# A transformer block with attention over channels and a gated convolution: strips without side columns, and the variance's epsilon on GpSimd

## The chip, the cores and the metric

The kernel runs on one core of one Trainium2 chip. The metric is the device time of one execution in microseconds (us). The engines are named as the profile names them: PE is TensorE (PEld its weight loads), DVE is VectorE, ACT is ScalarE, POOL is GpSimd, SP is SyncE, which only issues DMAs. All data is float32; one float32 matmul stands as two instructions in the trace.

## The reference, cut to what matters

`x` is 16 x 128 x 96 x 96 (batch, channels, height, width). Both LN weights are ones and both LN biases zeros in the data, but the kernel uses them as given.

```python
x_hwc = x.transpose(0, 2, 3, 1)
xn1 = _layernorm(x_hwc, ln1_w, ln1_b)            # over the 128 channels of a pixel, eps 1e-5
attn_out = _attention(xn1, wq, wk, wv, wp)       # 8 heads of 16 channels: a 16x16 matrix per head
x = x + attn_out.transpose(0, 3, 1, 2)
xn2 = _layernorm(x.transpose(0, 2, 3, 1), ln2_w, ln2_b).transpose(0, 3, 1, 2)
# _ffn: 1x1 conv 128 -> 512, depthwise 3x3 conv with zero padding, exact gelu, 1x1 conv 512 -> 128
x = x + _ffn(xn2, w_in, w_dw, w_out)
```

The attention normalizes q and k over all 9216 pixels, so it needs only the Gram matrix of the normalized pixels of an image; after that the whole attention is one 128x128 matrix and a column, applied to each pixel.

## The kernel before, in words

The images are worked through one after the other, the first norm of the next image overlapping the second half of this one. Pixels come in batches of four 128x128 tiles (576 batches in all: 18 of each image for the first norm `a`, 18 for the second norm `b`). For a batch, `forth` (L716) transposes the pixels on TensorE into one of two PSUM buffers (`tr`), `stats` (L723) takes mean and variance sums on VectorE, `variance` (L730) on ScalarE divides the sum by the 128 channels and adds epsilon, `power` (L734) on GpSimd raises to -1/2, `scaled` (L759) on ScalarE multiplies and writes the tile `zT`, `gram` (L768, first norm only) adds to the Gram matrix, `back` (L802) transposes back into the one buffer `bk`, and `place` (L805) copies it into a ring `xn` of rows. The mean is taken out in the weights. `attention` (L852 on) makes the 128x128 matrix, `mix` (L665) applies it.

The feed-forward part goes by blocks of 16 rows, 96 in all, and by four chunks of 128 hidden channels. For the first three chunks (`conv_job`) TensorE makes the hidden rows (`hidden`, L976), ScalarE keeps them with a bias (`kept`, L979), and the nine taps of the depthwise convolution are shared out: six on VectorE (`tap`, L1006, a scalar_tensor_tensor with two inputs in SBUF), two as products on ScalarE (`product`, L999) that DMAs issued by GpSimd add up (`add_products`, L1013), the centre tap in the first instruction. Then comes gelu (L1017).

The fourth chunk does the same in 25 blocks, and in the other 71 (`by_matmuls`, three blocks of four) the whole convolution runs on TensorE. There `split` (L1083) makes strips: for each of four groups of 32 channels, the four quarters of a PSUM bank hold odd or even rows and the left or right half of the width, nine rows of 49 columns and one column of the image's outer side, 50 columns in all. The outer column, and rows outside the image, are filled by matmuls of minus the bias (L1085). `kept` (L1092) copies all 450 columns to SBUF, and `conv` (L1105) multiplies by diagonal 64x32 tap matrices, four groups by two halves at a time. The tile `h1_3` is used for both kinds of block; when the kind goes from matmuls to taps, `around` (L439, L440) on GpSimd writes the zeros that the taps need.

`ffn_out` (L1139) multiplies back to 128 channels, ScalarE evicts (L1149), and a DMA adds to the output. All four PSUM banks `h` are shared by `hidden`, `split`, `conv`, `mix` and `ffn_out`.

The order of every engine's instructions is made ahead by `Plan`: each piece of work has an engine, a cost in ns, and a place (a number of jobs plus an offset of its kind from the table `AT`), and a simulated clock hands out the work that is ready in the order of places. `SLACK` is added to what a result takes to reach another engine, `STEP` spreads the pieces of one kind. On each engine the instructions then run in that fixed order, each waiting for its semaphores.

Of the kernel before, what the change touches and what calls it, by code (L numbers as in the profile page):

```python
# [39 lines left out]
    load_1=-318.45, load_2=250.75, tables=-176.75, weights=-199.9, zeros=280.85, pads=489.4, pads_0=-50.0,  # L40
    load_a=-397.35, forth_a=-242.55, stats_a=-48.4, variance_a=52.55, power_a=346.4, scaled_a=65.85,
    gram=-109.85, back_a=-291.7, place_a=163.65, attention=-399.95, mix=-263.75, residual=-1.05, mixed=-9.75,
    add_x=163.65, forth_b=-248.0, stats_b=-54.25, variance_b=-72.2, power_b=-242.45, shift_b=-65.25,
    scaled_b=519.65, back_b=-664.1, place_b=430.4, evicted=-175.6, add_out=-299.05, halo=332.2, hidden=-67.95,
    kept=-6.5, products=623.75, add_last=230.4, tap=-40.35, add_first=521.3, gelu=615.7, split=-72.5,
    packed=65.05, conv=-64.0, conv_gelu=-632.25, out=-63.65, add=699.15, store=57.0, mix_0=-629.3,
    residual_0=-0.45, mixed_0=1.1, add_x_0=-191.4, gram_0=425.2, forth_a_0=-164.1, forth_b_0=-555.1,
    stats_a_0=-203.2, stats_b_0=31.65, scaled_a_0=166.35, scaled_b_0=435.1, back_a_0=198.1, back_b_0=63.05,
    place_a_0=213.65, place_b_0=-41.2, shift_b_0=-104.65, late=436.35, store_x2=-259.8, store_x2_0=-280.3,
    variance_a_0=296.05, variance_b_0=-572.0, power_a_0=446.6, power_b_0=-200.95, attention_0=-700.85,  # L50
    load_a_0=-699.6, hidden_0=-343.05, kept_0=688.75, products_0=-317.3, tap_0=406.55, add_last_0=-476.1,
    add_first_0=-25.55, gelu_0=-695.0, split_0=-310.35, packed_0=-61.1, conv_0=-522.45, conv_gelu_0=2.7,
    out_0=-354.3, evicted_0=38.2,
# [3 lines left out]
STEP = dict(scaled=1.089, hidden=0.115, products=-0.129, tap=-0.536, split=2.985, conv=0.6, out=0.866)  # L57
SLACK = dict(PE=450, DVE=120, ACT=130, POOL=410, ADD=200, MOVE=360)
# [5 lines left out]
T_VARIANCE = 190  # L64
# [4 lines left out]
class Plan:  # L69
# [45 lines left out]
    def order(self):  # L115
# [39 lines left out]
        def dispatch(engine, time):  # L155
# [40 lines left out]
            elif engine == "POOL":  # L196
                rest = self.two - time
                ns, result = (ns, result) if rest <= 0 else (rest + ns - 143, rest + result - 143)
                own = result
# [49 lines left out]
def tile_restormer_block(  # L249
# [68 lines left out]
    def column(t, v):  # L318
# [5 lines left out]
    whole = const.tile([P, 1], F32, name="whole")  # L324
    nbeta = const.tile([P, P], F32, name="nbeta")
# [20 lines left out]
    SW, SR = W // 2 + 2, BR // 2 + 1  # L346
    PART = SR * SW
    h1s = [
        h1p.tile([P, (BR + 2) * WP + 2 if n != PE_CHUNK else 4 * PART], F32, name=f"h1_{n}") for n in range(NCH)
# [95 lines left out]
    def packed(k):  # L445
        return strips(h1s[PE_CHUNK][:, k * PART : (k + 1) * PART])
# [8 lines left out]
    def weights(p):  # L455
# [8 lines left out]
        def loads_1():  # L464
# [7 lines left out]
            v["col"] = t[:, 10 * P + Q : 10 * P + Q + 24].rearrange("p (a t) -> p a t", a=2)  # L472
            v["by_part"] = t[:, 11 * P : 11 * P + 48]
            v["nb"] = t[:, 11 * P + 48 : 11 * P + 49]
# [74 lines left out]
        def keep_in_centred():  # L549
            nc.scalar.copy(winT.rearrange("p n c -> p (n c)"), v["in_a"])  # L550
            nc.scalar.copy(beta, v["in_b"][:, P : P + NCH])

        def column_of():
# [20 lines left out]

        def diagonals():
            nc.vector.tensor_copy(v["by_part"], v["spread"])
# [72 lines left out]
    def norm(i, second, place_of):  # L649
# [49 lines left out]
        def pixels(s, m):  # L699
# [27 lines left out]
            def variance():  # L727
                d["mv"] = d["st"].rearrange("p j (t v) -> p (j t) v", v=3)
                ve = d["ve"] = small.tile([P, QB * QT], F32, tag="ve", name=f"ve_{name}_{m}")
                nc.scalar.activation(ve, d["mv"][:, :, 2], AF.Copy, scale=1.0 / C, bias=EPS)  # L730

            def power():
                rstd = d["rstd"] = small.tile([P, QB * QT], F32, tag="rstd", name=f"rstd_{name}_{m}")
                nc.gpsimd.tensor_tensor(rstd, d["ve"], mhalf, ALU.pow)  # L734
# [43 lines left out]
            act(T_VARIANCE, at("variance" + ab, s, i), variance, [(*bt, "s")], [(*bt, "r")])  # L778
# [45 lines left out]
    def attention(s, i):  # L824
# [26 lines left out]
        def _():  # L851
            nc.scalar.copy(sb([P, P + 1], "gs"), grams[i][:, : P + 1])  # L852
# [92 lines left out]
        def _():  # L945
            nc.scalar.copy(sb([P, P], "mwT", keep), v["ps_m"])
# [105 lines left out]
    def by_matmuls(p, g):  # L1052
# [15 lines left out]
        def split(k):  # L1068
            ph = d["ph", k] = bank((g, "split", k), PART)
            w = slice(k * Q, (k + 1) * Q)  # L1070
            todo, sides = [], []
            for q in range(4):
# [3 lines left out]
                for e in (*range(k0), *range(k1, SR)):  # L1076
                    sides.append(to[:, e, :])
                sides.append(to[:, k0:k1, half * (SW - 1)])
                lo, hi = (0, W // 2 + 1) if half == 0 else (W // 2 - 1, W)
                for e, (e0, m, z) in enumerate(strided(r0 - 1 + y + 2 * k0, k1 - k0)):  # L1080
                    todo.append((e, q, to[:, k0 + e0 : k0 + e0 + m, 1 - half : SW - half], z[:, :, lo:hi]))
# [166 lines left out]
```

## Time and profile before

| | |
|---|---|
| median of 3 runs | 3908.28 us (3907.63 to 3912.27) |
| the profiled execution | 3905.63 us, span 3903.9 us |
| TensorE busy | 3797.5 us, 97% |
| VectorE busy | 3695.5 us, 95% |
| ScalarE busy | 3618.6 us, 93% |
| GpSimd busy | 1858.0 us, 48% |
| granted TensorE clock, mean | 0.996 |

The span is the time from the first to the last instruction. A row of a group reads: line, engine, operation, what it writes and reads, how many, then busy time and mean duration in ns, then the idle time of the engine before them and what ended it. A row of the waits reads: who waited, for whom, the total in us, how often, the longest. A row of the timeline reads: start, duration, engine, line, operation, and in brackets the idle time before it. A GpSimd instruction's duration includes the time that it waits for the memory port.

### The profile page before, as it was taken

To read this page: it belongs to the slowest core of one execution; us is meant where nothing else is said; L and a number is where in the kernel's file an instruction comes from. 1 tells how busy PE (TensorE), PEld (TensorE's weight loads), DVE (VectorE), ACT (ScalarE), POOL (GpSimd) and SP (SyncE) were. 2 spreads that over 40 slices of the span, in tenths; PEclk is the share of its full clock that TensorE was granted. 3 is DMA by queue.
4 is the path that set the end of the run, shared out by engine and by line. 5 is a ranking of instruction groups with operands and counts; after the bars stand their busy time and mean duration, and the time that the engine had idled before them with its cause. 6 is when DMAs were issued, how large, how long until landed. Compare 5 with 4: busy or idle time off the path is not lost.

```text
span 3903.9 us, 81207 instructions
## 1 busy us (share of the span) xinstructions
PE 3797.5 (97%) x32452; PEld 2337.7 (60%) x32452; DVE 3695.5 (95%) x3310; ACT 3618.6 (93%) x7473; POOL 1858.0 (48%) x1586
## 2 busy tenths in 40 slices
PE   8899999999999999999999999999999999999998
PEld 6556656566565665656556565665656656666544
DVE  6998999999999999999999999999999999999998
ACT  6899999999999999999999999999999999899995
POOL 4445555354454545545445454544545444454431
PEclk9999999999999999999999999999999999999999
DMA  5899999999999999999999999999999999999997
GB/s 145 174 200 224 193 211 210 200 223 190 218 201 203 221 191 222 196 206 218 186 214 202 208 217 190 224 199 211 216 184 223 203 213 206 195 221 192 205 186 161
DMA packets 188921, 790.94 MB, mean 203 GB/s; under 512 B 21888, under 2 KB 23424, under 8 KB 188544
## 3 DMA queue, kind: packets, MB, share of 16 engines
q0 software_dynamic: 130608, 633.92, 83.7%
q1 hardware_dynamic: 57936, 151.83, 10.8%
q8 instruction: 256, 4.19, 0.4%
q14 instruction: 121, 0.99, 0.1%
HBM read 150.62 MB, written 149.42 MB: 77 GB/s over the span
## 4 chain that ended last, share of the span: by engine, by line
PE 58%; ACT 15%; DMA 10%; DVE 9%; issue 4%; POOL 3%; POOLq 0%; ACTq 0%; DVEq 0%; SPq 0%
PE h L1139 15%; PE h L976 12%; PE h L1105 10%; DMA h<-h 8%; DVE h L1006 8%; PE h L665 4%; PE g L768 4%; ACT h L999 4%; PE h L1083 4%; ACT h L979 3%; ACT zT L759 3%; PE pB_b L802 2%; PE pT_b L716 2%; PE pB_a L802 2%; ACT h L1017 2%
## 5 line engine op out<-in xcount | busy, mean ns | idle before, releaser
L1006 DVE SCALAR_TENSOR_TENSOR h<-h,ratio,h 128x1520 f32<-128x1520 f32 (+1 forms) x1567 | 2750.3, 1779 | 13.7
L1013 POOL DMA_DIRECT2D h<-h x624 | 589.7, 964 | 1045.3 <-ACT h L999 416.6
L1139 PE MATMUL h<-h,woutT 128*128 128x384 f32 x3072 | 1059.6, 489 | 11.1 <-ACT h L979 7.0
L999 ACT ACTIVATE h<-h,ratio 128x1536 f32<-128x1536 f32 (+1 forms) x624 | 1012.4, 1638 | 2.4 <-DMA h<-h 1.3
L976 PE MATMUL h<-xn,winT 128*128 128x384 f32 (+3 forms) x2466 | 947.8, 500 | 31.5 <-ACT h L1149 13.2
L1139 PEld LDWEIGHTS h<-h,woutT 128*128 128x128 f32 x3072 | 570.7, 191 | 389.5 <-issue 21.2
L979 ACT ACTIVATE h<-h,beta 128x384 f32<-128x384 f32 (+1 forms) x1204 | 734.1, 659 | 26.4 <-PE h L976 19.8
L734 POOL TENSOR_TENSOR rstd_a<-ve_a,mhalf 128x4 f32<-128x4 f32 x288 | 545.0, 1895 | 360.3 <-ACT ve_a L730 347.6
L734 POOL TENSOR_TENSOR rstd_b<-ve_b,mhalf 128x4 f32<-128x4 f32 x288 | 528.9, 1841 | 345.6 <-ACT ve_b L730 334.2
L1006 DVE SCALAR_TENSOR_TENSOR h<-h,ratio 128x1536 f32<-128x1536 f32 x313 | 567.0, 1812 | 95.8 <-ACT h L979 94.7
L1105 PE MATMUL h<-h,taps 64*32 64x384 f32 x13632 | 584.7, 484 | 2.3 <-ACT h L979 2.3
L976 PEld LDWEIGHTS h<-xn,winT 128*128 128x128 f32 x2466 | 419.0, 190 | 232.6 <-ACT h L1149 26.6
L1017 ACT ACTIVATE h<-h 128x1536 f32<-128x1536 f32 (+1 forms) x316 | 484.5, 1534 | 32.6 <-DMA h<-h 31.8
L1105 PEld LDWEIGHTS h<-h,taps 64*32 64x32 f32 x13632 | 251.0, 106 | 288.5 <-issue 260.2
L759 ACT ACTIVATE zT<-pT_b,rstd_b 128x128 f32<-128x128 f32 x1132 | 338.0, 440 | 9.3 <-POOL rstd_b L734 8.4
L759 ACT ACTIVATE zT<-pT_a,rstd_a 128x128 f32<-128x128 f32 x1080 | 319.8, 421 | 18.1 <-POOL rstd_a L734 18.0
L768 PE MATMUL g<-zT 128*128 128x129 f32 x2160 | 286.8, 275 | 3.9 <-ACT zT L759 3.9
L665 PE MATMUL h<-xn,mwT 128*128 128x384 f32 x768 | 279.2, 490 | 3.2 <-ACT x L674 2.9
L768 PEld LDWEIGHTS g<-zT 128*128 128x128 f32 x2160 | 263.7, 191 | 6.7 <-ACT zT L759 4.3
L1149 ACT COPY h<-h 128x384 f32<-128x384 f32 x376 | 201.3, 535 | 60.9 <-PE h L1139 60.2
L1083 PE MATMUL h<-xn,winT 128*32 128x441 f32 (+4 forms) x2464 | 250.4, 507 | 1.7 <-ACT h L1113 1.7
L723 DVE BATCH_NORM_STATS2 st_b<-pT_b 128x6 f32<-128x256 f32 x566 | 211.9, 419 | 28.4 <-PE pT_b L716 19.3
(190 smaller groups left out, 3776.3 us busy)
## 6 DMA issues: line engine op xcount, KB each, us to landing
h<-h POOLq DMA_DIRECT2D x520, 768.0 KB, 9.5
h<-h POOLq DMA_DIRECT2D x104, 720.0 KB, 10.5
x<-in_x_dram SPq DMA_DIRECT2D x192, 384.0 KB, 7.5
out_dram<-x SPq DMA_DIRECT2D x190, 384.0 KB, 9.3
x<-in_x_dram POOLq DMA_DIRECT2D x189, 384.0 KB, 9.2
out_dram<-h POOLq DMA_DIRECT2D x94, 768.0 KB, 10.7
out_dram<-x SPq DMA_DIRECT2D x4, 192.0 KB, 1.9
h<-in_L_conv_w_in_dram SPq DMA_DIRECT2D x1, 256.0 KB, 2.7
```

Source lines behind the costliest of these rows:

```text
L665: nc.tensor.matmul(rows(pm), lhsT=mats[i][0], rhs=interior(i, u), start=True, stop=True)
L734: nc.gpsimd.tensor_tensor(rstd, d["ve"], mhalf, ALU.pow)
L759: nc.scalar.activation(zT(q)[:, k, :P], d["pT", q][:, k, :], AF.Copy, scale=d["rstd"][:, t : t + 1])
L768: nc.tensor.matmul(grams[i][:, : P + 1], lhsT=zt[:, :P], rhs=zt, start=(q == 0 and k == 0), stop=(q == NU * TPU // QT - 1 and k == QT - 1),)
L976: nc.tensor.matmul(rows(ph)[:, k : k + m, :], lhsT=winT[:, n, :], rhs=z, start=True, stop=True)
L979: nc.scalar.activation(window(h1_, r, e - r, 1), rows(d.pop(("ph", r))), AF.Identity, bias=beta[:, n : n + 1])
L999: nc.scalar.activation(d["pr", t][:, o0:o1, :], shifted(t, o0, o1), AF.Copy, scale=ratio[:, n, t : t + 1])
L1006: nc.vector.scalar_tensor_tensor(h3[:, o0:o1, w0:w1], shifted(t, o0, o1, w0, w1), ratio[:, n, t : t + 1], onto, ALU.mult, ALU.add)
L1013: nc.gpsimd.dma_start(out=to[:, o0:o1, :], in_=d["pr", t][:, o0:o1, :], accum_op=ALU.add)
L1017: nc.scalar.activation(h3, h3, AF.Gelu)
L1105: nc.tensor.matmul(halves(d["pc", y, c][k * Q : (k + 1) * Q, :]), lhsT=taps[cs, k, 6 * y + t, :], rhs=packed(k)[cs, up : up + SR - 1, dx : ...
L1139: nc.tensor.matmul(rows(d["po"]), lhsT=woutT[:, n, :], rhs=h3s[g, n][:, s * UR : (s + 1) * UR, :], start=(k == 0), stop=(k == NCH - 1),)
```

## The change

The strips lose their outer column: `SW` is 49, `split` fills nine rows of 49 with no side matmuls, and the copies move 441 columns. In SBUF the rows of a part stand 50 apart and share one side column between the end of a row and the start of the next; that column holds minus the bias and is written by GpSimd (`sides`, four instructions of 128x10) each time the kind of block goes from taps to matmuls, 25 times. Of 1320 matmuls with minus the bias, 184 remain, for rows outside the image.

The variance step is now a GpSimd instruction of 128x4 ahead of the power, 576 of each. It only adds 128 times epsilon to the sum of squares; the missing division by 128 is made up by factors in the weights and in the copies of the attention, where one copy becomes two (16 instructions more on ScalarE). Costs, slacks and all places in the tables are new, and so is the order on every engine.

```diff
-    SW, SR = W // 2 + 2, BR // 2 + 1
-    PART = SR * SW
+    SW, SR = W // 2 + 1, BR // 2 + 1
+    PART = SR * (SW + 1) + 1
...
-    def packed(k):
-        return strips(h1s[PE_CHUNK][:, k * PART : (k + 1) * PART])
+    def packed(k, r, n, at_, m):
+        o = k * PART + r * (SW + 1) + at_
+        return h1s[PE_CHUNK][:, o : o + n * (SW + 1)].rearrange("p (r w) -> p r w", w=SW + 1)[:, :, :m]
+
+    def sides():
+        for k in range(4):
+            nc.gpsimd.tensor_scalar(
+                h1s[PE_CHUNK][:, k * PART : (k + 1) * PART : SW + 1], ones_row[:, : SR + 1], npad[:, k : k + 1], None, ALU.mult
+            )
...
             def variance():
                 d["mv"] = d["st"].rearrange("p j (t v) -> p (j t) v", v=3)
-                ve = d["ve"] = small.tile([P, QB * QT], F32, tag="ve", name=f"ve_{name}_{m}")
-                nc.scalar.activation(ve, d["mv"][:, :, 2], AF.Copy, scale=1.0 / C, bias=EPS)
+                rstd = d["rstd"] = small.tile([P, QB * QT], F32, tag="rstd", name=f"rstd_{name}_{m}")
+                nc.gpsimd.tensor_scalar(rstd, d["mv"][:, :, 2], C * EPS, None, ALU.add)
 
             def power():
-                rstd = d["rstd"] = small.tile([P, QB * QT], F32, tag="rstd", name=f"rstd_{name}_{m}")
-                nc.gpsimd.tensor_tensor(rstd, d["ve"], mhalf, ALU.pow)
+                nc.gpsimd.tensor_tensor(d["rstd"], d["rstd"], mhalf, ALU.pow)
...
-            act(T_VARIANCE, at("variance" + ab, s, i), variance, [(*bt, "s")], [(*bt, "r")])
+            op("POOL", T_VARIANCE, at("power" + ab, s, i), variance, [(*bt, "s")], [(*bt, "r")], T_VARIANCE, T_VARIANCE)
...
-            nc.scalar.copy(sb([P, P + 1], "gs"), grams[i][:, : P + 1])
+            gs = sb([P, P + 1], "gs")
+            nc.scalar.activation(gs[:, :P], grams[i][:, :P], AF.Copy, scale=float(C))
+            nc.scalar.activation(gs[:, P:], grams[i][:, P : P + 1], AF.Copy, scale=C**0.5)
...
-                sides.append(to[:, k0:k1, half * (SW - 1)])
-                lo, hi = (0, W // 2 + 1) if half == 0 else (W // 2 - 1, W)
+                lo, hi = (0, SW) if half == 0 else (W - SW, W)
...
-            nc.scalar.copy(packed(k), strips(d.pop(("ph", k))))
+            nc.scalar.copy(packed(k, 0, SR, 1, SW), strips(d.pop(("ph", k))))
...
-                if not by_pe(g):
-                    pool(300, at("pads", first[g], g >= HEAD), lambda: around(h1s[PE_CHUNK]), [], [*whole_h1, ("pk",)])
+                change = sides if by_pe(g) else lambda: around(h1s[PE_CHUNK])
+                pool(700 if by_pe(g) else 300, at("pads", first[g], g >= HEAD), change, [("w", "conv")], [*whole_h1, ("pk",)])
...
-SLACK = dict(PE=450, DVE=120, ACT=130, POOL=410, ADD=200, MOVE=360)
+SLACK = dict(PE=9, DVE=228, ACT=4, POOL=453, ADD=949, MOVE=44)
```

What this moves on the engines is seen in the order of their instructions. On TensorE before, in the middle of an image, a pair of strips (here written to the banks h_76 and h_78), its side matmuls, and what follows:

```order
L768 MATMUL g_3279<-zT_150 128x129 x4
L1083 MATMUL h_76<-xn,winT 32x9x49 x4
L1085 MATMUL h_76<-ones_row,nbeta 32x9 x4
L1083 MATMUL h_78<-xn,winT 32x9x49 x4
L1085 MATMUL h_78<-ones_row,nbeta 32x9 x4
L858 MATMUL g_3279<-wqkT,gs_4674 128x256
```

and at such a place in the changed kernel, where both pairs of a block follow each other:

```order
L1093 MATMUL h_79<-xn,winT 32x441 x4
L1093 MATMUL h_78<-xn,winT 32x441 x4
L1093 MATMUL h_76<-xn,winT 32x441 x4
L1093 MATMUL h_77<-xn,winT 32x441 x4
L1149 MATMUL h_79<-h_12_146,woutT 128x384
```

The side matmuls are gone, and the next work stands right behind the strips.

On GpSimd before, in the second norm (`rstd_b` are its powers, the DMAs with `h` add the products of taps, L677 adds x, L1153 adds to the output):

```order
L734 TENSOR_TENSOR rstd_b_2_9442<-ve_b_2_9439,mhalf 128x4
L1013 DMA h_7_140<-h_6_139 128x1440
L677 DMA x_4_5_9434<-in_x_dram 128x768
L734 TENSOR_TENSOR rstd_b_3_9475<-ve_b_3_9469,mhalf 128x4
L1153 DMA out_dram<-h_8_141 128x1536
L734 TENSOR_TENSOR rstd_b_4_9520<-ve_b_4_9516,mhalf 128x4
```

and after, where both norms and the four instructions of `sides` (L452) meet:

```order
L740 TENSOR_SCALAR rstd_b_8_5075<-st_b_8_5062 128x4
L743 TENSOR_TENSOR rstd_b_8_5075<-rstd_b_8_5075,mhalf 128x4
L687 DMA x_2_9_5066<-in_x_dram 128x768
L452 TENSOR_SCALAR h_3_133<-ones_row,npad 128x10 x4
L1024 DMA h_10_144<-h_1_135 128x1440
L1024 DMA h_0_134<-h_13_147 128x1536
L740 TENSOR_SCALAR rstd_a_1_5143<-st_a_1_5136 128x4
L743 TENSOR_TENSOR rstd_a_1_5143<-rstd_a_1_5143,mhalf 128x4
```

Each power now has an instruction ahead of it that waits for the statistics themselves, mostly with nothing between the two, and two DMAs of tap products stand behind the four sides.

More of the change, by code (lines that the diff above doesn't have):

```diff
@@ L45 @@
[L45 to L49, printed above, removed]
@@ new lines @@
+    gram=210.95, back_a=-266.95, place_a=-700.0, attention=-230.4, mix=39.5, residual=-1.05, mixed=395.6,
+    add_x=-48.55, forth_b=146.8, stats_b=-444.3, variance_b=-72.2, power_b=219.9, shift_b=-65.25,
+    scaled_b=-160.4, back_b=-668.3, place_b=144.05, evicted=-688.8, add_out=83.65, halo=692.3, hidden=317.1,
+    kept=-136.65, products=412.4, add_last=-539.35, tap=-104.2, add_first=-440.95, gelu=249.75, split=-194.25,
+    packed=-622.2, conv=321.6, conv_gelu=-402.05, out=323.9, add=-349.15, store=116.65, mix_0=-436.95,
@@ L56 @@
 Q = 32
-STEP = dict(scaled=1.089, hidden=0.115, products=-0.129, tap=-0.536, split=2.985, conv=0.6, out=0.866)
-SLACK = dict(PE=450, DVE=120, ACT=130, POOL=410, ADD=200, MOVE=360)
+STEP = dict(scaled=0.202, hidden=0.107, products=0.662, tap=0.151, split=-0.021, conv=1.084, out=-0.853)
+SLACK = dict(PE=9, DVE=228, ACT=4, POOL=453, ADD=949, MOVE=44)
 NORM1_END = 6.0
@@ L197, in dispatch @@
                 rest = self.two - time
-                ns, result = (ns, result) if rest <= 0 else (rest + ns - 143, rest + result - 143)
-                own = result
+                if rest > 0:
+                    ns, result, own = rest + ns - 143, rest + result - 143, rest + own - 143
             if o[9]:
@@ L324, in tile_restormer_block @@
     whole = const.tile([P, 1], F32, name="whole")
+    npad = const.tile([P, NCH], F32, name="npad")
     nbeta = const.tile([P, P], F32, name="nbeta")
@@ L342, in tile_restormer_block @@
     h1p = ctx.enter_context(tc.tile_pool(name="h1p", bufs=1))
-    SW, SR = W // 2 + 2, BR // 2 + 1
-    PART = SR * SW
+    SW, SR = W // 2 + 1, BR // 2 + 1
+    PART = SR * (SW + 1) + 1
     h1s = [
-        h1p.tile([P, (BR + 2) * WP + 2 if n != PE_CHUNK else 4 * PART], F32, name=f"h1_{n}") for n in range(NCH)
+        h1p.tile([P, (BR + 2) * WP + 2 if n != PE_CHUNK else 4 * PART + 4], F32, name=f"h1_{n}") for n in range(NCH)
     ]
@@ L945, in _ @@
         def _():
-            nc.scalar.copy(sb([P, P], "mwT", keep), v["ps_m"])
+            nc.scalar.activation(sb([P, P], "mwT", keep), v["ps_m"], AF.Copy, scale=C**0.5)
             nc.scalar.copy(sb([P, 1], "d", keep), v["ps_d"])
@@ L1068, in split @@
         def split(k):
[L1069 removed]
+            ph = d["ph", k] = bank((g, "split", k), SR * SW)
             w = slice(k * Q, (k + 1) * Q)
[L1071 removed]
+            todo, outside = [], []
             for q in range(4):
```

50 lines of the change are left out of this document (26 added, 24 removed).

## The prediction

> **What bounds the kernel now.** I read the head of the page first, then the busy time in four stretches, then the waits of TensorE. The page's head gives the span and the work of each engine.
>
> ```profile
> span 3903.9 us, 81207 instructions
> PE 3797.5 (97%) x32452; PEld 2337.7 (60%) x32452; DVE 3695.5 (95%) x3310; ACT 3618.6 (93%) x7473; POOL 1858.0 (48%) x1586
> ```
>
> Three engines are nearly full, so the average cannot say which one sets the pace. The stretches can (start, end and length, then the busy time of each engine, the granted clock and the share of the DMA engines):
>
> ```profile
> 0.00:170.00 170.00, 141.93 (x1024) 98.59 (x1027) 130.36 (x217) 129.60 (x325) 77.30 (x104) 0.95 0.69 162
> 170.00:600.00 430.00, 418.62 (x3520) 257.43 (x3520) 410.07 (x363) 404.57 (x833) 212.81 (x175) 1.00 0.95 205
> 600.00:3600.00 3000.00, 2959.88 (x25677) 1832.23 (x25662) 2868.16 (x2520) 2839.93 (x5895) 1472.63 (x1215) 1.00 0.97 207
> 3600.00:3903.90 303.90, 277.06 (x2254) 149.46 (x2253) 286.86 (x213) 244.48 (x423) 95.27 (x94) 0.98 0.91 183
> ```
>
> In the 3000 us of the middle TensorE is idle for 40.1 us, VectorE for 131.8, ScalarE for 160.1. The clock is granted in full. TensorE is the bound there, at 98.7%; over the whole span its idle time is 3903.9 - 3797.5 = 106.4 us, 66 of it at the two ends. What makes it idle in the middle is ScalarE:
>
> ```profile
> PE h L976 <- ACT h L1149: 11.3, 13, 1.8
> PE g L858 <- ACT gs L852: 5.7, 6, 2.4
> PE h L976 <- ACT h L1113: 4.6, 6, 0.8
> PE g L768 <- ACT zT L759: 3.9, 5, 0.9
> PE pT_a L716 <- ACT zT L759: 3.4, 7, 0.5
> PE pT_b L716 <- ACT zT L759: 3.0, 7, 0.8
> ```
>
> These six are 31.9 of the 40.1 us, each wait short. So a gain has to come from less work on TensorE, or from ScalarE answering it sooner, and a loss from anything that makes TensorE wait again.
>
> **First part: the side columns leave TensorE.** Of the 1320 matmuls that fill sides and outside rows, 184 stay (outside rows): 71 blocks x 16 = 1136 go. Each is two instructions in the trace. The group rows, and one pair of strips in the timeline:
>
> ```profile
> L1085 PE MATMUL h<-ones_row,nbeta 128*32 128x9 f32 (+2 forms) x2640 | 75.0, 179 | 0.0
> 1368.86 0.95 PE L1083 MATMUL h<-xn,winT 128*32 128x441 f32 x8
> 1369.63 0.22 PE L1085 MATMUL h<-ones_row,nbeta 128*32 128x9 f32 x8
> 1369.68 0.93 PE L1083 MATMUL h<-xn,winT 128*32 128x441 f32 x8
> 1370.43 0.22 PE L1085 MATMUL h<-ones_row,nbeta 128*32 128x9 f32 x8
> 1370.58 0.55 PE L802 MATMUL pB_a<-ident,zT 128*128 128x128 f32 x3
> ...
> 1330.02 2.74 PE L1139 MATMUL h<-h,woutT 128*128 128x384 f32 x8
> 1332.60 0.49 PE L802 MATMUL pB_a<-ident,zT 128*128 128x128 f32 x3
> ...
> 1740.61 4.10 PE L1105 MATMUL h<-h,taps 64*32 64x384 f32 x96
> 1744.65 0.55 PE L802 MATMUL pB_b<-ident,zT 128*128 128x128 f32 x3
> ```
>
> The 75.0 us are not the price: the side matmuls overlap the strips. A pair takes 1370.58 - 1368.86 = 1.72 us until the next matmul starts. Eight passes of 384 columns take 2.58 us, 0.3225 each, so one of 441 takes 0.370 and the pair's four passes (four column groups side by side) 1.48. That leaves 0.24 us for the sides and for the change of the tile shape. The convolution has that change without sides: its twelve passes take 4.04 us against 12 x 0.3225 = 3.87, so 0.17 us are the change's. The sides' own price is then between 0.24 - 0.17 = 0.07 us and 0.24 us a pair, and over 142 pairs between 10 and 34 us. The two sit close to the lower row, and I take 0.10 us: **-14 us**. The eviction of a strip shrinks from 450 to 441 columns, under 3 us of ScalarE in all, which I cost at nothing on the path.
>
> **Second part: the variance leaves ScalarE for GpSimd.** The rows of the two operations now, the wait for the result, and a stretch of VectorE, GpSimd and ScalarE:
>
> ```profile
> L734 POOL TENSOR_TENSOR rstd_a<-ve_a,mhalf 128x4 f32<-128x4 f32 x288 | 545.0, 1895 | 360.3 <-ACT ve_a L730 347.6
> L730 ACT ACTIVATE ve_b<-st_b 128x4 f32<-128x4 f32 x288 | 79.1, 280 | 22.1 <-DVE st_b L723 21.1
> L730 ACT ACTIVATE ve_a<-st_a 128x4 f32<-128x4 f32 x288 | 76.6, 270 | 10.6 <-DVE st_a L723 9.8
> ...
> 1323.72 1.79 DVE L1006 SCALAR_TENSOR_TENSOR h<-h,ratio,h 128x1520 f32<-128x1520 f32 x1
> 1326.11 1.78 DVE L1006 SCALAR_TENSOR_TENSOR h<-h,ratio,h 128x1520 f32<-128x1520 f32 x1
> 1327.81 0.75 DVE L723 BATCH_NORM_STATS2 st_a<-pT_a 128x6 f32<-128x256 f32 x2
> 1328.48 5.45 DVE L1006 SCALAR_TENSOR_TENSOR h<-h,ratio,h 128x1520 f32<-128x1520 f32 x3
> ...
> 1324.30 0.12 POOL L439 MEMSET h<- 128x18 f32 x1 [2.80 <-PE h L1105]
> 1326.88 1.90 POOL L734 TENSOR_TENSOR rstd_b<-ve_b,mhalf 128x4 f32<-128x4 f32 x1 [2.45 <-ACT ve_b L730]
> 1329.48 1.68 POOL L734 TENSOR_TENSOR rstd_a<-ve_a,mhalf 128x4 f32<-128x4 f32 x1
> ...
> 1330.94 1.15 ACT L759 ACTIVATE zT<-pT_b,rstd_b 128x128 f32<-128x128 f32 x4
> ...
> 1337.19 1.20 ACT L759 ACTIVATE zT<-pT_a,rstd_a 128x128 f32<-128x128 f32 x4
> ```
>
> 576 of ScalarE's 7473 instructions go, 79.1 + 76.6 = 156 us of its 3618.6 busy; in the middle its load falls from 0.947 to about 0.906. That is off the bound, and it pays only through the 40.1 us in which TensorE waits. Its bounds are 0 (the order of the evictions makes the waits, not the load) and -32 (all six rows vanish). Since ScalarE loses one instruction in thirteen and the waits are short, I take a fifth of 40.1: **-8 us**. The second copy in the attention's first step adds 16 small ScalarE instructions behind which TensorE waits (the row of L858); at 0.28 us each, what the smallest ScalarE rows here take, that is +4.5 us at most, and I take +1.
>
> Now the other side. The power that began at 1326.88 ended at 1328.78, 0.89 us after the tap that ended at 1327.89; the one from 1329.48 ended at 1331.16, 0.90 us after the first of the three taps (5.45 / 3 = 1.8 us each) was over. A power thus waits for the end of the running tap and then needs 0.9 us. The memset, which reads nothing, took 0.12 us in the middle of a tap. The new epsilon instruction reads, so I take it to wait like the power and to run like the memset, 0.12 us. It starts right behind the statistics, just as the next tap starts, and so waits for nearly a whole one; the power behind it may find the tap after that already running. In the stretch above that gives 1327.89 + 0.12 + 0.9 = 1328.9 for the first batch (0.1 us later than now, as statistics follow the tap) and 1328.48 + 2 x 1.8 + 0.9 = 1333.0 for the second (1.8 later). Their scaled copies started at 1330.94 and 1337.19, 2.2 and 6.0 us after the power. So most batches have room for up to 1.8 us. The bounds of the term: below nothing, since the hop over ScalarE is gone (0.92 us from the end of the statistics at 1328.56 to the power at 1329.48) and TensorE's 10.3 us of waits for zT could shrink; above, the rival below. I take **+3 us**.
>
> The Trainium skill, SBUF — State Buffer, section "Who interferes with whom", says that a VectorE instruction with two SBUF inputs contends with a GpSimd instruction that reads SBUF and not with one that only writes. The taps have two such inputs, and the trace agrees on both counts (0.9 us behind the tap, 0.12 us inside one). Its section "SBUF: two separate sides" goes further: whichever starts first holds the port for its whole instruction. By that, each new GpSimd read would also hold up a tap; the trace does not show it, for the three taps with a power inside took 5.45 us, 1.82 each, against 1.79 and 1.78 for those alone, and the sum has no term for it.
>
> On GpSimd's queue the epsilon is an added 576 x 0.12 us without waits and up to 576 x 1.9 with them, 70 to 1090 us on an engine at 48%. Behind it stand the DMA issues for the tap products. Their transfers keep the DMA engines 97% busy in the middle, so an issue that comes 1.8 us late meets a queue that still has work; I cost it at nothing, and at up to 3% of a stretch if that backlog is gone.
>
> **Third part: the sides written once.** 25 times, where a block by matmuls follows one by taps, GpSimd makes four instructions of 128x10. They read, so each may wait for a tap: 4 x 0.12 = 0.5 us at the least, 4 x 1.9 = 7.6 at the most, 190 us of GpSimd in all. They start when the last tap on this block's buffer is over, and TensorE waits for them before the first convolution of the block alone. The evictions of the strips stand between the two, and they too need that tap to be over:
>
> ```profile
> L1092 ACT COPY h<-h 128x450 f32<-128x450 f32 x284 | 153.2, 596 | 2.3 <-DVE h L1006 2.0 <-PE h L1085 0.2
> ```
>
> Four of them are 2.2 us of cover at the least; that all 284 waited for taps only 2.0 us says that they come well after the tap, so the cover is larger, and I take 0. With the least cover it is up to 25 x (7.6 - 2.2) = 135 us, which would need the four to wait for a tap each and the convolution to follow at once.
>
> **The new order** moves everything else. It adds no work, and of its effect on the waits of TensorE the trace says only that there are 106 us to lose or win; I take 0 and 20 us to either side.
>
> **The sum** against the profiled execution, 3905.6 us (span 3903.9): -14 - 8 + 1 + 3 = -18, so 3887.6. The median of the runs is 3908.3, 2.7 above the profiled one: **3890 us**.
>
> **The rivals.**
> *The scaled copies come too late (slower).* Two transpose buffers serve 576 batches, and a buffer is free only after the scaled copy. Net of the hop that is gone, a late batch is 1.8 - 0.9 = 0.9 us later. If TensorE waits that long for one batch in ten, that is 58 x 0.9 = 52 us, and ScalarE's relief is lost with it: 3908.3 - 14 + 1 + 52 = 3947 us. It decides against the change from 23 batches on (20 / 0.9). For it: one GpSimd instruction more in a chain that now ends 3 to 4 us behind the statistics, and short waits for zT already there. Against it: the room of 2.2 and 6.0 us. Chance 0.24.
> *The work removed was not the limit (no change).* DMA stands at 0.97, VectorE at 0.956 of the middle; if the transfers or the taps pace TensorE, 14 us turn into idle time and the rest is unmoved: 3908 us. For it: the three shares; against it: TensorE's waits name ScalarE, not DMA or VectorE. The same time comes out if the sides were wholly hidden, so that the change does not take from TensorE what it says. Chance 0.16.
> *ScalarE's relief pays in full.* All six rows of waits go and the sides are worth half their upper bound: 3908.3 - 32 - 17 + 1 = 3860 us. Chance 0.12.
>
> **How the numbers follow.** The forecast has 0.48. Its own range is 3890 with 20 us to either side for the order, 3870 to 3910, which reaches a little into no change. For eight times in ten I go to 3856 below, just under the full relief, and to 3930 above, which holds the milder half of the late copies. A difference under 0.2%, 7.8 us, can't be told from none here. Faster: 0.48 x 0.95 + 0.12 + 0.16 x 0.1 = 0.59, rounded to 0.60; the same 0.16; slower 0.24.
>
> **What would show it.** Right: the side matmuls' row at about 368 instructions, the time between a pair's start and the next matmul near 1.62 us, TensorE's busy time near 3783, its idle time at or under 106, ScalarE's busy time near 3460. The epsilon's row should have a mean between 0.12 and 1.9 us. Wrong: if TensorE's waits for zT rise from about 10 us to over 30, if the convolution waits for GpSimd, or if its idle time passes 125 us.

## The result: slower by 3.2%

The changed kernel takes 4035.51 us (median of 4 runs, 4032.51 to 4036.53); the kernel before, run beside it, 3910.24 us. The ratio is 1.0319, 95% interval 1.0302 to 1.0337. That is 125 us slower where 18 us faster were forecast, and it lies outside the range of 3856 to 3930.

The head of the page of the changed kernel, and its busy time in three of the four stretches of the prediction and in its last 135 us (columns as there):

```profile
span 4034.8 us, 77166 instructions
PE 3838.5 (95%) x30180; PEld 2323.8 (58%) x30180; DVE 3708.0 (92%) x3312; ACT 3579.5 (89%) x6913; POOL 2661.3 (66%) x2262
```

```profile
0.00:170.00 170.00, 136.79 (x793) 92.77 (x794) 125.70 (x210) 118.16 (x260) 106.76 (x141) 0.89 0.64 150
170.00:600.00 430.00, 414.59 (x3222) 253.00 (x3221) 391.33 (x351) 385.26 (x752) 294.98 (x240) 0.98 0.92 197
600.00:3600.00 3000.00, 2899.45 (x23183) 1763.07 (x23189) 2800.30 (x2457) 2733.39 (x5313) 2043.29 (x1703) 1.00 0.95 202
3900.00:4034.80 134.80, 103.22 (x786) 52.80 (x770) 108.10 (x69) 71.48 (x97) 49.09 (x27) 0.91 0.70 144
```

TensorE has fewer instructions and yet stands for 100.6 of the middle 3000 us, where it stood for 40.1. VectorE's work is the same in both kernels, so its count of instructions shows progress: 2457 in these 3000 us against 2520, which is 63 / 2457 x 3000 = 77 us lost there. In the first 600 us it did 561 against 580, about 20 us. The rest of the 131 us between the two profiled spans, some 34 us, is lost at the end.

By TensorE's own account, 90 of the 131 us are more idle time (196 us against 106) and 41 are more busy time, though it has 2272 instructions fewer. Its granted clock was lower on the mean, 0.985 against 0.996; what else makes its busy time longer stays open. GpSimd's busy time rose by 803 us, from 1858.0 to 2661.3.

How much of the end hangs on GpSimd, the chain of work that ended last tells, first of the kernel before, then of the changed one:

```profile
PE 58%; ACT 15%; DMA 10%; DVE 9%; issue 4%; POOL 3%; POOLq 0%; ACTq 0%; DVEq 0%; SPq 0%
```

```profile
PE 45%; POOL 17%; ACT 12%; DVE 10%; issue 7%; DMA 2%; POOLq 0%; DVEq 0%; ACTq 0%
```

GpSimd's share went from 3% to 17%. The groups of the changed kernel say what it does in that time: L740 is the epsilon, L743 the power, L452 the sides, L1095 the side matmuls that are left.

```profile
L740 POOL TENSOR_SCALAR rstd_b<-st_b 128x4 f32<-128x4 f32 x288 | 353.6, 1228 | 250.2 <-DVE st_b L733 237.7 <-ACT zT L768 12.4
L740 POOL TENSOR_SCALAR rstd_a<-st_a 128x4 f32<-128x4 f32 x288 | 320.5, 1113 | 158.9 <-DVE st_a L733 157.5 <-ACT xn L814 1.1
L743 POOL TENSOR_TENSOR rstd_a<-rstd_a,mhalf 128x4 f32<-128x4 f32 x288 | 544.8, 1892 | 21.9
L452 POOL TENSOR_SCALAR h<-ones_row,npad 128x10 f32<-128x10 f32 x100 | 182.4, 1841 | 7.5 <-DVE h L1017 7.5
L1095 PE MATMUL h<-ones_row,nbeta 128*32 128x49 f32 x368 | 24.3, 205 | 0.0
```

An epsilon takes 1.1 to 1.2 us on the mean, and the power behind it 1.9 us again, as before. One of the sides takes 1.79 us in the median; the mean of 1.84 holds one of 30.2 us, of which the last section tells. The waits of the changed kernel show who pays (whole span; who waited, for whom, total, times, longest):

```profile
ACT zT L768 <- POOL rstd_b L743: 63.8, 50, 4.7
ACT zT L768 <- POOL rstd_a L743: 57.8, 42, 4.0
PE pB_b L811 <- ACT xn L814: 41.5, 40, 4.9
PE pB_a L811 <- ACT xn L814: 26.8, 26, 3.6
PE pT_b L726 <- ACT zT L768: 19.2, 33, 2.4
```

ScalarE stands 121.6 us at the scaled copies, where the kernel before stood 26.4 (the sum of these two rows):

```profile
ACT zT L759 <- POOL rstd_a L734: 18.0, 18, 2.3
ACT zT L759 <- POOL rstd_b L734: 8.4, 13, 1.4
```

Its order is fixed, so the copy `place` (L814) behind a scaled copy comes late too. TensorE's `back` (L811) waits for `place` because there is only one buffer `bk`: 68.3 us, where it was 21.0:

```profile
PE pB_b L802 <- ACT xn L805: 17.0, 7, 4.7
PE pB_a L802 <- ACT xn L805: 4.0, 8, 1.6
```

In the middle 3000 us alone it is 52.4 us (27.6 and 24.8) against 2.5 (0.7 and 1.8), most of the 60.5 us by which TensorE's idle time rose there. That is the chain: late power, late scaled copy, late `place`, idle TensorE.

One batch of each norm in the timeline of the changed kernel, on GpSimd and then on ScalarE (start, duration, engine, line):

```profile
1588.55 2.12 POOL L740 TENSOR_SCALAR rstd_a<-st_a 128x4 f32<-128x4 f32 x1
1590.75 1.04 POOL L743 TENSOR_TENSOR rstd_a<-rstd_a,mhalf 128x4 f32<-128x4 f32 x1
1591.79 1.27 POOL L740 TENSOR_SCALAR rstd_b<-st_b 128x4 f32<-128x4 f32 x1
1593.14 2.34 POOL L743 TENSOR_TENSOR rstd_b<-rstd_b,mhalf 128x4 f32<-128x4 f32 x1
...
1591.82 1.14 ACT L768 ACTIVATE zT<-pT_a,rstd_a 128x128 f32<-128x128 f32 x4 [0.89 <-POOL rstd_a L743]
```

Two reads in a row for a batch take 3.2 us (1588.55 to 1591.79) where one took 1.7 to 1.9 in the prediction's stretch; ScalarE started its copy 0.03 us after the power ended, with 0.89 us of standing before it. That batch had no room at all. The second batch's pair stood behind the first on GpSimd's queue and ended at 1595.48.

### The profile page after: what moved, and what is told of

It reads as the page before. It is cut to its first block, busy times and chain, and to the rows that moved or that the text cites. A ratio compares the mean times of both kernels' runs of the same rounds, so it can differ in the third digit from the quotient of the medians.

```text
span 4034.8 us, 77166 instructions
## 1 busy us (share of the span) xinstructions
PE 3838.5 (95%) x30180; PEld 2323.8 (58%) x30180; DVE 3708.0 (92%) x3312; ACT 3579.5 (89%) x6913; POOL 2661.3 (66%) x2262
## 4 chain that ended last, share of the span: by engine, by line
PE 45%; POOL 17%; ACT 12%; DVE 10%; issue 7%; DMA 2%; POOLq 0%; DVEq 0%; ACTq 0%
PE h L1149 12%; PE h L1115 8%; PE h L987 8%; DVE h L1017 8%; POOL rstd_b L743 4%; PE h L675 4%; PE h L1093 3%; ACT zT L768 3%; POOL rstd_a L743 3%; PE g L777 3%; POOL h L452 3%; POOL h L1024 2%; ACT h L1010 2%; ACT h L990 2%; POOL rstd_b L740 2%
## 5 line engine op out<-in xcount | busy, mean ns | idle before, releaser
L1017 DVE SCALAR_TENSOR_TENSOR h<-h,ratio,h 128x1520 f32<-128x1520 f32 (+1 forms) x1567 | 2750.5, 1780 | 14.4
L1149 PE MATMUL h<-h,woutT 128*128 128x384 f32 x3072 | 1061.0, 489 | 11.3 <-ACT h L990 5.8
L1010 ACT ACTIVATE h<-h,ratio 128x1536 f32<-128x1536 f32 x624 | 1004.3, 1635 | 17.4 <-DMA h<-h 11.2
L987 PE MATMUL h<-xn,winT 128*128 128x384 f32 (+3 forms) x2466 | 933.1, 501 | 28.4 <-ACT h L1123 11.2
L1024 POOL DMA_DIRECT2D h<-h x624 | 579.5, 979 | 576.3 <-ACT h L1010 209.2
L990 ACT ACTIVATE h<-h,beta 128x384 f32<-128x384 f32 (+1 forms) x1204 | 712.8, 655 | 51.6 <-PE h L987 21.1
L1115 PE MATMUL h<-h,taps 64*32 64x384 f32 x13632 | 589.3, 485 | 11.5 <-POOL h L452 10.8
L987 PEld LDWEIGHTS h<-xn,winT 128*128 128x128 f32 x2466 | 431.4, 192 | 264.6 <-issue 55.4
L743 POOL TENSOR_TENSOR rstd_a<-rstd_a,mhalf 128x4 f32<-128x4 f32 x288 | 544.8, 1892 | 21.9
L743 POOL TENSOR_TENSOR rstd_b<-rstd_b,mhalf 128x4 f32<-128x4 f32 x288 | 534.7, 1856 | 18.4
L740 POOL TENSOR_SCALAR rstd_b<-st_b 128x4 f32<-128x4 f32 x288 | 353.6, 1228 | 250.2 <-DVE st_b L733 237.7
L740 POOL TENSOR_SCALAR rstd_a<-st_a 128x4 f32<-128x4 f32 x288 | 320.5, 1113 | 158.9 <-DVE st_a L733 157.5
L675 PE MATMUL h<-xn,mwT 128*128 128x384 f32 x768 | 291.3, 502 | 18.7 <-ACT h L990 10.7
## 6 DMA issues: line engine op xcount, KB each, us to landing
h<-h POOLq DMA_DIRECT2D x104, 720.0 KB, 10.3
```

The source lines that it names most:

```text
L740: nc.gpsimd.tensor_scalar(rstd, d["mv"][:, :, 2], C * EPS, None, ALU.add)
L743: nc.gpsimd.tensor_tensor(d["rstd"], d["rstd"], mhalf, ALU.pow)
L987: nc.tensor.matmul(rows(ph)[:, k : k + m, :], lhsT=winT[:, n, :], rhs=z, start=True, stop=True)
L990: nc.scalar.activation(window(h1_, r, e - r, 1), rows(d.pop(("ph", r))), AF.Identity, bias=beta[:, n : n + 1])
L1010: nc.scalar.activation(d["pr", t][:, o0:o1, :], shifted(t, o0, o1), AF.Copy, scale=ratio[:, n, t : t + 1])
L1017: nc.vector.scalar_tensor_tensor(h3[:, o0:o1, w0:w1], shifted(t, o0, o1, w0, w1), ratio[:, n, t : t + 1], onto, ALU.mult, ALU.add)
```

## The experiments

Twelve kernels were run. The expectations weigh theory P, the port: each added GpSimd instruction that reads waits for the end of a tap, and the queue behind it waits along; theory L, by which the loss sits in the chain of the norms; and the new order by itself. (In the expectations, O is the new order, S the sides alone, and Q a plan that any shift against it upsets.) Ratios are to the kernel before on the same chip, with 95% intervals.

| kernel | median us | ratio |
|---|---|---|
| the change | 4035.51 | 1.0319 (1.0302 to 1.0337) |
| e1, epsilon on ScalarE in the new order | 4014.15 | 1.0268 (1.0249 to 1.0286) |
| e2, old order, variance on GpSimd | 4020.36 | 1.0288 (1.0272 to 1.0303) |
| e3, new order, no epsilon | 3961.70 | 1.0136 (1.0120 to 1.0153) |
| e4, old order, strips, sides as in the change | 3998.15 | 1.0227 (1.0211 to 1.0242) |
| e5, new order, sides by memset | 3966.22 | 1.0150 (1.0135 to 1.0165) |
| e8, old order, strips, sides by memset | 3894.05 | 0.9968 (0.9954 to 0.9982) |
| e9, old order, strips, sides by one ScalarE copy | 3897.91 | 0.9972 (0.9960 to 0.9984) |
| e10, new order, memset and no epsilon | 3911.47 | 1.0009 (1.0000 to 1.0019) |
| e11, old order, memset ahead of the power | 3897.40 | 0.9973 (0.9963 to 0.9983) |
| e12, e9 with its one copy on GpSimd | 3927.43 | 1.0052 (1.0037 to 1.0067) |
| e13, e9 with its order made anew | 3961.38 | 1.0140 (1.0125 to 1.0155) |
| e14, e11 with a read in place of the memset | 3976.67 | 1.0179 (1.0162 to 1.0196) |

### The epsilon: e1, e2, e3

e1 puts the added instruction back on ScalarE and leaves every place in the order as it is:

```diff
-                nc.gpsimd.tensor_scalar(rstd, d["mv"][:, :, 2], C * EPS, None, ALU.add)
+                nc.scalar.activation(rstd, d["mv"][:, :, 2], AF.Copy, bias=C * EPS)
```

> The changed kernel, its plan and order kept, but the epsilon of the variance is added by ScalarE again, at the place in the order where the GpSimd instruction stood; GpSimd has the power alone. Theory L (late rstd: on GpSimd the epsilon and then the power each wait for the end of a VectorE tap, rstd comes late, ScalarE stands at its scaled copy and everything behind it is late): the waits of ScalarE for rstd fall from 122 us to about 20, and the time to 3900 to 3940 us. Theory O (the new order itself has work for TensorE too close behind what ScalarE must evict, whoever adds the epsilon): 4000 to 4050 us. Theory S (the sides, written by GpSimd in four instructions that each wait for a tap, hold up what stands behind them): 4000 to 4050 us.

It gained only 21 us, to 4014.15: L's number was missed, and the time is one that O and S allow. The scaled copies still waited 80.6 us for the power (42.1 and 38.5). A likely reason is ScalarE's hop, which this order had not provided for; this run does not separate it.

e2 is the other half: the kernel before, with its own order, and the whole variance on GpSimd right ahead of the power.

```diff
-                nc.scalar.activation(ve, d["mv"][:, :, 2], AF.Copy, scale=1.0 / C, bias=EPS)
...
+                nc.gpsimd.tensor_scalar(ve, d["mv"][:, :, 2], 1.0 / C, EPS, ALU.mult, ALU.add)
                 nc.gpsimd.tensor_tensor(rstd, ve, mhalf, ALU.pow)
```

> The kernel before, every engine's order kept, but the epsilon instruction leaves ScalarE and stands on GpSimd right ahead of its power (division by 128 and epsilon in one instruction). Strips as before. Theory L: the second wait comes with it, 3950 to 4030 us. Theory O: ScalarE is 156 us freer and the order is the old one, 3890 to 3920 us. Theory S: as O.

4020.36 us: this move alone costs 113 us in the old order. Its waits of ScalarE:

```profile
ACT zT L759 <- POOL rstd_a L734: 94.9, 84, 4.6
ACT zT L759 <- POOL rstd_b L734: 82.0, 48, 3.7
```

176.9 us at the scaled copies against 26.4. It is the same place as in the changed kernel, without its order and without its strips, so neither O nor S can be the whole of it.

e3 leaves the epsilon out of the changed kernel; the power reads the statistics.

```diff
-                nc.gpsimd.tensor_scalar(rstd, d["mv"][:, :, 2], C * EPS, None, ALU.add)
...
-                nc.gpsimd.tensor_tensor(d["rstd"], d["rstd"], mhalf, ALU.pow)
+                nc.gpsimd.tensor_tensor(d["rstd"], d["mv"][:, :, 2], mhalf, ALU.pow)
```

> The changed kernel, its order kept, without the epsilon instruction: the power reads the statistics directly, and epsilon is left out of the result (a part of 100000 of the variance). Neither ScalarE nor GpSimd has an instruction for it. Theory L: the chain has one wait for a tap, 3890 to 3930 us. Theory O and theory S: 4000 to 4040 us, little less than the changed kernel.

3961.70 us, 74 less than the change. That is a large part, and 53 us over the kernel before stay. The time lies between the two forecasts: neither L nor O and S explain it alone.

### The sides: e4, e5, e8

e4 makes only the strips, in the old order. The four GpSimd instructions are issued right ahead of the copy of the first strip.

```diff
+            if k == 0 and (g == 0 or not by_pe(g - 1)):
+                sides()
             nc.scalar.copy(packed(k, 0, SR, 1, SW), strips(d.pop(("ph", k))))
```

> The kernel before, its order kept, with the strips of the change alone: no side matmuls in the 71 blocks, copies of 441 columns, sides written by GpSimd 25 times (issued just ahead of the first copy of such a block). Variance on ScalarE. Theories L and O: TensorE has 14 us less to do, 3890 to 3905 us. Theory S: 3960 us or more, with the convolution or the power waiting behind the sides.

3998.15 us: the part of the change that takes 1136 matmuls from TensorE makes the kernel some 90 us slower by itself. L's number was missed. The row of the sides (25 x 4; shortest, median, longest in ns), and of the waits of ScalarE those for DMA and GpSimd:

```profile
L452 POOL TENSOR_SCALAR h<-ones_row,npad x100: 312/1748/21385, 137.3 to 3931.1; 128x10 f32<-128x10 f32 x100
```

```profile
ACT h L1027 <- DMA h<-h: 53.9, 37, 4.8
ACT zT L769 <- POOL rstd_b L744: 39.0, 20, 4.5
ACT zT L769 <- POOL rstd_a L744: 34.9, 17, 9.2
```

In the middle of the distribution one takes 1.75 us, so four hold GpSimd's queue for 7 us. What is late is not the convolution above all (TensorE waited 13.7 us for the sides) but what stands behind them on that queue: the power (73.9 us of waits against 26.4) and the issues of the DMAs that add the tap products. The gelu (L1027) waited 53.9 us for those DMAs; before, it was 31.8:

```profile
ACT h L1017 <- DMA h<-h: 31.8, 22, 5.8
```

e8 is e4 with four instructions that only write. They write zeros, which is minus the bias in this data only.

```diff
-            nc.gpsimd.tensor_scalar(
-                h1s[PE_CHUNK][:, k * PART : (k + 1) * PART : SW + 1], ones_row[:, : SR + 1], npad[:, k : k + 1], None, ALU.mult
-            )
+            nc.gpsimd.memset(h1s[PE_CHUNK][:, k * PART : (k + 1) * PART : SW + 1], 0.0)
```

> The kernel before with the strips alone and its order kept, as in the run that took 3998 us, but the sides are memsets (zeros, right with these data). Theory P: the 91 us vanish and the 14 us of side matmuls stay gone, 3885 to 3905 us. Theory Q: TensorE still runs ahead of the plan, 3960 us or more.

3894.05 us. With the same number of instructions at the same places on the same queue, what is gone is their reading, and 104 us with it. The strips' own gain shows now: 0.32%, 12.5 us (7 to 18 by the interval).

e5 is the same edit in the changed kernel:

> The changed kernel, its order kept, with the four side instructions of each switch as memsets, which only write (they write zeros, which is what minus the bias is with these data; another bias would need its value). Theory P (port: every GpSimd instruction added that reads the memory waits for the end of a tap, and the queue behind it waits too): the sides' 25 x 4 waits go, one wait of 30 us near the end among them, 3940 to 3990 us, with the epsilon's waits left. Theory Q (plan: any shift against the durations that the order was made for costs as much): within 15 us of 4035.

3966.22 us, 69 less than the change: nearly the same as the epsilon's 74.

### Reading or being one more: e11 and e14

Two kernels in the old order without ScalarE's variance (the factors as in the change, the epsilon left out). In e11 a GpSimd memset, on which nothing depends, stands ahead of each power; e14 puts in its place an instruction that reads a constant, on which nothing depends either.

```diff
-                nc.gpsimd.memset(ve, 0.0)
+                nc.gpsimd.tensor_scalar(ve, mhalf, C * EPS, None, ALU.add)
                 nc.gpsimd.tensor_tensor(rstd, d["mv"][:, :, 2], mhalf, ALU.pow)
```

> The order before, strips as before; ScalarE's variance instruction is gone, and ahead of each power GpSimd has a memset of 128x4 in place of the epsilon; the power reads the statistics directly (epsilon is left out of the result; the division by 128 is in the weights and copies as in the changed kernel). So GpSimd has as many instructions as in the run that took 4020 us, but the added one reads nothing and waits for no port. Theory P: 3880 to 3910 us. Theory Q: 3950 us or more.

> As the run with a GpSimd memset ahead of each power in the order before (3897 us; no variance instruction on ScalarE, epsilon left out of the result), but the added instruction reads a constant of 128x4 and writes a tile that nobody uses, so it stands in no chain of data. Theory P (port and queue): it waits for a tap each time and holds up the power behind it, 3960 to 4020 us. If the price lay in the longer chain of data (statistics, epsilon, power), it stays at 3890 to 3910 us.

e11: 3897.40 us, 11 us faster than the kernel before. e14: 3976.67 us, 79 us slower than e11. The rows of the added instruction and of the power behind it in e14:

```profile
L733 POOL TENSOR_SCALAR ve_b<-mhalf 128x4 f32<-128x4 f32 x288 | 400.3, 1390 | 0.0
...
L734 POOL TENSOR_TENSOR rstd_b<-st_b,mhalf 128x4 f32<-128x4 f32 x288 | 628.3, 2206 | 119.1 <-DVE st_b L723 119.1
```

and in e11:

```profile
L734 POOL TENSOR_TENSOR rstd_b<-st_b,mhalf 128x4 f32<-128x4 f32 x288 | 594.2, 2077 | 241.5 <-DVE st_b L723 240.2 <-PE pB_b L802 0.6 <-PE h L978 0.4
...
L733 POOL MEMSET ve_b<- 128x4 f32 x288 | 131.5, 457 | 0.0
```

The memset took 0.46 us on the mean, the read 1.39. GpSimd had 240 us of idle time ahead of these powers in e11 and half of it in e14. e2, whose added instruction also carries the data, is 44 us above e14. So the epsilon's 123 us in the old order (e2 against e11) are 79 for one more read on the queue and, by difference, 44 for standing in the chain of the data.

### The order, and a version that is faster: e10, e9, e12, e13

e10 takes both causes out of the changed kernel: the edits of e3 and e5 together.

> The changed kernel, its order kept, with both sources of port waits gone: the sides are memsets (zeros, right with these data) and the epsilon instruction is left out (epsilon missing from the result). What is left of the change is the new order, the side matmuls that are gone and the ScalarE instruction that is gone. Theory P: the two single removals gave 69 and 74 us; together 4035 - 143 = 3892 us, within 15, so the new order as such is worth about nothing. Theory O (the new order has its own price): 3930 us or more.

3911.47 us, ratio 1.0009 (1.0000 to 1.0019): the two edits together give back 124 us. Singly they gave 74 and 69, so 19 us of the two overlap. It is 4 us above what theory P allowed, 3892 us within 15. The scaled copies' wait is back under its old 26.4 us, in one row, and so is TensorE's at `back`, 20.8 us (18.0 and 2.8):

```profile
ACT zT L766 <- POOL rstd_b L741: 18.3, 18, 1.6
```

But e10 has the strips (worth 12.5 us in e8) and no variance on ScalarE (worth 11 in e11), and should then be near 3885. The 27 us between are the new order's, if the parts add, which no run shows by itself. They are lost in part at the end: by 3600 us VectorE has done 3104 instructions in e10 and 3098 in the kernel before, and yet e10's profiled execution ends 2 us later.

e9 writes the sides, with the bias as given, by one copy on ScalarE:

```diff
-        for k in range(4):
-            nc.gpsimd.tensor_scalar(
-                h1s[PE_CHUNK][:, k * PART : (k + 1) * PART : SW + 1], ones_row[:, : SR + 1], npad[:, k : k + 1], None, ALU.mult
-            )
+        to = h1s[PE_CHUNK][:, : 4 * PART].rearrange("p (k e) -> p k e", e=PART)[:, :, :: SW + 1]
+        nc.scalar.copy(to, npad.unsqueeze(2).to_broadcast([P, NCH, SR + 1]))
```

> The same strips in the order before, but the sides of a switch are one ScalarE copy of 128x4x10 just ahead of the first strip's copy, general in the bias; GpSimd has nothing to do with them. Theory P: 3885 to 3905 us, as with memsets. Theory Q: 3960 us or more.

3897.91 us, 0.9972: faster than both kernels, by 0.28% of the kernel before, and by its code for any bias. The 25 copies take 9.2 us of ScalarE in all. A pair of strips in its timeline:

```profile
1368.63 1.69 PE L1090 MATMUL h<-xn,winT 128*32 128x441 f32 x16
1370.25 0.55 PE L810 MATMUL pB_a<-ident,zT 128*128 128x128 f32 x3
```

1370.25 - 1368.63 = 1.62 us until the next matmul, where it was 1.72.

e12 is e9 with that one copy on GpSimd (`nc.gpsimd.tensor_copy` for `nc.scalar.copy`), so one read in place of four:

> The strips in the order before, the sides of a switch written by one GpSimd copy of 128x4x10 that reads, in place of four instructions (3998 us) or four that only write (3894 us). Theory P (the price goes by the number of waits for a tap): about a quarter of 104 us, 3910 to 3930 us. If the price is that of any reading at all, 3980 us or more.

3927.43 us, 30 us above e9 and 71 below e4. It is not a clean count of reads: here the strip copies themselves wait for GpSimd, which in e4 they did not. Of the waits of ScalarE in e12:

```profile
ACT h L1101 <- POOL h L452: 40.1, 18, 19.2
```

The powers are on time again (the scaled copies waited 8.2 and 6.1 us for them), and what is lost is that direct wait, 19.2 of its 40.1 us in one place near the end.

e13 gives the strips of e9 their true, shorter costs in the plan, so that the order comes out anew:

```diff
-            pe(2 * t_mm(450) + 230, at("split", pk, g >= HEAD), lambda k=k: splits((k, k + 1)), [*zs, ("w", "conv"), ("w", "in")], [*phs, ("pk",)])
+            pe(2 * t_mm(SR * SW) + 150, at("split", pk, g >= HEAD), lambda k=k: splits((k, k + 1)), [*zs, ("w", "conv"), ("w", "in")], [*phs, ("pk",)])
...
-                act(t_copy(450), at("packed", pk, g >= HEAD), lambda k=k + e: kept(k), [phs[e]], parts[k + e])
+                act(t_copy(SR * SW), at("packed", pk, g >= HEAD), lambda k=k + e: kept(k), [phs[e]], parts[k + e])
```

> The strips in the kernel before with the sides by one ScalarE copy (3898 us), the tables of places as before, but the plan is given the shorter costs of strips and copies and makes its order anew. A try for a faster kernel. Theory P gives no port waits, so 3870 to 3910 us; if a new order by itself costs what the changed kernel lost, 3950 us or more.

3961.38 us, 64 us above e9 with the same instructions. That is not P's 3870 to 3910 us but the time named for an order that costs something by itself. The scaled copies waited 25.0 us for the power, so late powers are not in it. TensorE's waits in the middle are spread over many rows, of which these are the longest three:

```profile
PE h L1114 <- ACT h L987: 10.7, 5, 3.3
PE pT_a L724 <- ACT zT L767: 7.6, 10, 3.3
PE pB_b L810 <- ACT xn L813: 5.3, 8, 1.4
```

So an order that nobody has chosen by its time on the chip can lose 64 us with the same work.

## Why the prediction was wrong

**What bounded the kernel before** was read rightly as far as the parts that take work away go: both of them paid about what the sum said. How full ScalarE was, was misread, as told below.

**The side matmuls, -14 us:** right. 368 instructions are left, the pair takes 1.62 us as forecast (in e9), and e8 measured -12.5.

**ScalarE's relief, -8 us:** right in size. e11 has the relief, the second copy in the attention, the hop over ScalarE gone and no read added, and measured -11 (-7 to -14). The fifth of TensorE's waits that the sum took was a guess, so the agreement is in part luck. The load under it was misread: the variance's rows add up to 156 us, but without them ScalarE's busy time fell by 40, from 3618.6 to 3578.4 in e11 (3579.5 in the changed kernel, where 3460 was forecast). The rows of all its groups add up to some 4400 us in the kernel before, more than its busy time: its instructions overlap in the trace, as the side matmuls do.

**The norm's chain, +3 us:** this is the first step that failed. The mechanism was there, the epsilon's mean of 1.1 to 1.2 us lies in the forecast's 0.12 to 1.9, and "a late batch" was priced. What failed is what it made of "most batches have room for up to 1.8 us". Most had: in the changed kernel the scaled copies waited 92 times, in 576 batches. But these 92 waits are 121.6 us, and the sum took the batches without room for nearly nothing. The room was read from two batches (2.2 and 6.0 us), one short stretch of one image; the scaled copies' own rows of waits, 31 short waits in the trace of before, said that some batches had none. The term measured 74 us in the new order (the change less e3) and 123 us in the old one (e2 less e11). The step also counted only the batch's own chain: by e14, 79 of the 123 us come from a read that carries no data, by holding GpSimd's queue.

**GpSimd's queue and the sides, 0:** the second step that failed, as large as the first. The price of the four reads was right at its upper end, 4 x 1.9 = 7.6 us:

```profile
1247.06 7.47 POOL L452 TENSOR_SCALAR h<-ones_row,npad 128x10 f32<-128x10 f32 x4 [0.92 <-DVE h L1017]
1254.47 2.72 POOL L1024 DMA_DIRECT2D h<-h  x3
1256.19 1.76 POOL L917 TENSOR_TENSOR rn<-n,mhalf 128x2 f32<-128x2 f32 x1
```

The cover was the error. The prediction looked for who waits for the sides' result, found the convolution and four evictions, and that held: in the changed kernel TensorE waited once, 10.8 us, for the sides. But what 7.5 us on GpSimd delay is the whole queue behind them, here three DMA issues and a power in the attention. The bound of 135 us was of the right size and was dismissed for the wrong reason. Measured: 104 us in the old order (e4 less e8), 69 in the new one.

**The new order, 0 ± 20 us:** too narrow. e10 leaves about +27 for it, and e13, another order for the same instructions, lost 64. Which steps of the order cost this stays open.

**The rival "the scaled copies come too late"** had the mechanism and the sign. Its price, 52 us, was too low for that chain (74 us in the new order, 123 in the old): ScalarE waited 92 times for 1.3 us on the mean, before 31 times for 0.9. It expected TensorE to stand at the transposes; it stood more at `back`, whose one buffer waits for `place` behind the late scaled copy. And it did not contain the sides.

**The signs.** Two of the prediction's signs of "wrong" came out: TensorE's idle time is 4034.8 - 3838.5 = 196 us, over 125, and the convolution waited for GpSimd, once. The third did not: TensorE's waits for zT, 10.3 us in the middle, are 11.3 there in the changed kernel (9.5, 1.1 and 0.7); it stood at `back` instead. Of the signs of "right", TensorE's busy time was to be near 3783 and is 3838.5; without the two kinds of reads, in e10, it is 3787.9.

**The rule on the port.** The Trainium skill, SBUF — State Buffer, "Who interferes with whom", separates GpSimd instructions that read from those that only write beside a VectorE instruction with two SBUF inputs. The runs agree: e14 against e11 (+79 us) and e4 against e8 (+104 us) differ only in the added instructions, which read in the one and only write in the other. Of its section "SBUF: two separate sides", by which a GpSimd read would in turn hold up a tap, the runs show nothing. The taps' rows of the kernel before and of the change:

```profile
L1006 DVE SCALAR_TENSOR_TENSOR h<-h,ratio,h 128x1520 f32<-128x1520 f32 (+1 forms) x1567 | 2750.3, 1779 | 13.7
```

```profile
L1017 DVE SCALAR_TENSOR_TENSOR h<-h,ratio,h 128x1520 f32<-128x1520 f32 (+1 forms) x1567 | 2750.5, 1780 | 14.4
```

With 676 reads more on GpSimd the taps take the same 1.78 us, with 14.4 us of idle time ahead of them against 13.7. The prediction's choice to have no term for it was right.

## What to carry to other kernels

On an engine that works through a fixed queue, an added instruction is priced by what stands behind it on that queue, not only by who reads its result; low busy time (48% here) is no cover when each of its results is wanted soon. A GpSimd instruction that reads, beside VectorE instructions with two SBUF inputs, waits as a rule for the end of the running one, however small it is, and several small ones wait several times; one that only writes does not, and another engine with a copy of 0.4 us may be the better place. Room for lateness should be counted over all batches, from the rows of waits, not read from a stretch.

## What the runs showed that was not expected

A read on GpSimd was as a rule let in when the running tap ended. Near the end of four kernels it was not: the timeline of the changed kernel, GpSimd and then VectorE:

```profile
3944.92 31.08 POOL L452 TENSOR_SCALAR h<-ones_row,npad 128x10 f32<-128x10 f32 x4
3975.94 2.63 POOL L1024 DMA_DIRECT2D h<-h  x3
...
3945.66 1.81 DVE L1017 SCALAR_TENSOR_TENSOR h<-h,ratio 128x1536 f32<-128x1536 f32 x1
3947.39 6.93 DVE L1017 SCALAR_TENSOR_TENSOR h<-h,ratio,h 128x1520 f32<-128x1520 f32 x4
3954.24 1.81 DVE L1017 SCALAR_TENSOR_TENSOR h<-h,ratio 128x1536 f32<-128x1536 f32 x1
3955.97 10.36 DVE L1017 SCALAR_TENSOR_TENSOR h<-h,ratio,h 128x1520 f32<-128x1520 f32 x6
3966.25 1.81 DVE L1017 SCALAR_TENSOR_TENSOR h<-h,ratio 128x1536 f32<-128x1536 f32 x1
3967.98 6.93 DVE L1017 SCALAR_TENSOR_TENSOR h<-h,ratio,h 128x1520 f32<-128x1520 f32 x4
```

The first of the four alone stood for 30.2 us, to 3975.12, past the 17 taps shown (1 + 4 + 1 + 6 + 1 + 4), and the other three took 0.9 us together once the run of taps had ended (3967.98 + 6.93 = 3974.91). In e3, which has the same order, one took 30.2 us again, in e4 one took 21.4 and in e12 the single copy 16.2:

```profile
L452 POOL COPY h<-npad x25: 274/992/16180, 137.0 to 3831.9; 128x40 f32<-128x40 f32 x25
```

In all four the wait ended 0.1 to 0.2 us after the first gap in VectorE's taps. The taps there follow without a gap, each starting some 85 ns before the end of the one before is recorded. But one tap of the stretch at 1247 us ran into the next in the same way, and the read behind it was let in. What decides it was not tried and stays open.
